# Spreading the taps' weights by transfers and ScalarE copies instead of matmuls, in the first layer of a four-layer network

## The chip, the cores and the metric

The kernel runs on one core of a Trainium2 chip. The metric is the time of one execution on the device, in microseconds (us); the kernel before takes 5737.23 us, the median of three executions (5730.73 to 5739.15).

A core has several engines, each of which works through its own list of instructions in order: TensorE (PE: matmuls into the banks of PSUM), VectorE (DVE), ScalarE (ACT), GpSimd (POOL) and SyncE (SP), which here issues the transfers that the DMA engines carry out. They wait for each other through semaphores. Everything is in float32.

## The reference, cut to what matters

The input x has the shape (2, 512, 64, 64). Four layers follow each other; each adds to x a function of the group-normalized x. Only the first layer is touched by the change. It is an attention in which each of 4096 positions of an image, in each of 8 heads of 64 channels, looks at its 3x3 neighbourhood (9 *taps*) and at 256 pooled tokens:

```python
q_norm = _l2norm(q)
q_scaled = (q_norm + query_embedding[None]) * jax.nn.softplus(temperature)[None]
k_l = _l2norm(k_l.reshape(B, N, nh, hd)).reshape(B, N, C)
# ... k_local, v_local: the 9 shifted images of keys and values
attn_local = jnp.einsum('bhnd,bhndk->bhnk', q_scaled, k_local)
attn_pool = jnp.einsum('bhnd,bhpd->bhnp', q_scaled, _l2norm(k_pool))
attn = jax.nn.softmax(jnp.concatenate([attn_local, attn_pool], axis=-1), axis=-1)
a_local, a_pool = (attn[..., :ll], attn[..., ll:])
lt = jnp.einsum('bhnd,hdk->bhnk', q_norm, learnable_tokens) + learnable_bias[None] + a_local
x_local = jnp.einsum('bhnk,bhndk->bhnd', lt, v_local)
x_pool = jnp.einsum('bhnp,bhpd->bhnd', a_pool, v_pool)
out = ((x_local + x_pool).transpose(0, 2, 1, 3).reshape(B, N, C) @ W_proj + b_proj)
```

Two steps matter here. In x_local each of the 9 weights of a head and a position (lt) multiplies 64 channels of the shifted values, so one row of weights has to be *spread* over 64 partitions. And q and k are divided by their norms, for which 1/sqrt of a sum of squares is needed.

## The kernel before

The first layer works in *units*: two heads (128 channels, one on each partition) by 1024 positions. An image has 4 x 4 = 16 units, both images 32. In each round of the main loop several units are in work at different stages; the stages are Python generators that are advanced in turn, one step of each, and this decides the order of the instructions on every engine:

```python
UT = 2 * TB          # TB = 512: a unit is 1024 positions, two blocks
...
for i in range(-4, units + 1):
    k, q, ahead, u, before = (unit(i + n) for n in (4, 3, 1, 0, -1))
    streams, ended = [], []
    stages = [self.norms(streams, ended)]
    if before is not None:
        stages.append(self.weigh(before))          # apply the taps' weights of the unit before
    if ahead is not None:
        stages.append(self.tap_products(ahead))
    if u is not None:
        stages.append(self.attend(u))              # softmax and pooled part of this unit
    if ahead is not None:
        stages.append(self.tap_sums(ahead))
    stages.append(self.projections(k, q, ahead, streams))
    stages.append(self.normed(ended))
    # ... the output projection, beside the last rounds
    in_turn(*stages)
```

PSUM has a ring of five banks of 128x512 for all these stages ("mm", `self.bank()`), two banks for qs and one for the tap sums.

The attention's stage ends with the reciprocal of the softmax's sums, and the unit's weights are applied in the next round. The spread is a matmul with a matrix of zeros and ones (tapb) from 18 rows of weights to 128 partitions; VectorE multiplies the bank by the shifted values, and GpSimd adds the product to the output:

```python
def attend(self, u):
    # ... exponentials, values, sums (psD) of the unit
    for i in range(2):
        part = slice(i * TB // 2, (i + 1) * TB // 2)
        nc.vector.reciprocal(self.recip[:, part], psD[:, part])
    yield
    yield

def weigh(self, u):
    nc = self.nc
    cc, y0 = u // self.UN, u % self.UN * self.UY
    out, R = self.out.pop(u), self.recip
    el, lt = self.el.pop(u), self.lt.pop(u)
    yield
    banks = [self.bank() for _ in range(2)]
    for j, ps in enumerate(banks):
        q = slice(64 * j, 64 * j + 2)
        nc.tensor.matmul(ps, self.cst[q, C_ROW:C_ROW + P], R[q, :], start=True, stop=True)
    nc.vector.tensor_tensor(el, el, R, ALU.mult)
    nc.vector.tensor_tensor(el, el, lt, ALU.add)
    for j, ps in enumerate(banks):
        o = out[:, j * TB:(j + 1) * TB]
        nc.vector.tensor_tensor(o, o, ps, ALU.mult)
    yield
    for k in range(0, 9, 2):
        banks = {}
        for kk in range(k, min(k + 2, 9)):
            for j in range(2):
                q = 2 * j + kk % 2
                banks[kk, j] = ps = self.bank()
                nc.tensor.matmul(ps, self.tapb[32 * q:32 * q + 18, kk, :],     # L2203
                                 el[32 * q:32 * q + 18, :], start=True, stop=True)
        for (kk, j), ps in banks.items():
            dy, dx = divmod(kk, 3)
            dst = self.weighed[kk % 2]
            y = y0 + dy + j * self.UY // 2
            nc.vector.tensor_tensor(                                           # L2209
                dst[:, j * TB:(j + 1) * TB].rearrange("p (y x) -> p y x", x=W),
                self.vx[:, y:y + self.UY // 2, dx:dx + W],
                ps.rearrange("p (y x) -> p y x", x=W), ALU.mult)
            o = out[:, j * TB:(j + 1) * TB]
            nc.gpsimd.tensor_tensor(o, o, dst[:, j * TB:(j + 1) * TB], ALU.add) # L2214
        yield
        if k < 6:
            yield
    lo = u % self.UN * self.UT
    nc.sync.dma_start(self.yd[:, cc, lo:lo + self.UT], out)
    yield
```

The norms' roots are taken by one instruction on GpSimd, a power of -0.5 on 128x32 elements, once a round:

```python
n = wp.tile([P, NT, 4, 2], F32, name="norms")
nc.vector.tensor_scalar(n, ps.rearrange("p (t s r) -> p t s r", t=NT, s=4)[:, :, :, :2],
                        1e-24, None, ALU.max)                                  # L2012
yield
nc.gpsimd.tensor_tensor(                                                       # L2015
    self.wide.rearrange("p t (s r) -> p t s r", s=4)[:, :, :, :2], n,
    self.half.rearrange("p (t s h) -> p t s h", t=NT, s=4), ALU.pow)
yield
yield
# ... transposes of self.wide, a copy, and the multiplications of q and k
```

Of the kernel before, what the change touches and what calls it, by code (L numbers as in the profile page):

```python
# [8 lines left out]
F32 = mybir.dt.float32  # L9
I32 = mybir.dt.int32  # L10
AF = mybir.ActivationFunctionType
ALU = mybir.AluOpType
# [3 lines left out]
P = 128  # L16
C = 512
KC = C // P
W = 64
N = W * W  # L20
TB = 512
NB = N // TB
NT = TB // P
NH = 8
HD = 64
# [16 lines left out]
def bcast(ap, axis, n):  # L42

    a = ap.unsqueeze(axis)
    shape = list(a.shape)
    shape[axis] = n
    return a.to_broadcast(shape)
# [1612 lines left out]
class Local:  # L1660
# [9 lines left out]
    def __init__(self, net, X, Y, sp_scale, d, wp, yp, pp, ppt, pps):  # L1670
# [5 lines left out]
        self.yd = yp.tile([P, KC, N], F32, name="yd")  # L1676
        self.wd = yp.tile([3, P, KC, C], F32, name="wd")

        R = W + 2
# [5 lines left out]
        weighed = whole.take([P, 2 * self.UT])  # L1685
        self.weighed = [weighed[:, i * self.UT:(i + 1) * self.UT] for i in range(2)]
        self.prods = [whole.take([P, self.UT])] + [new([P, self.UT], f"prod{i}") for i in range(2)]
# [21 lines left out]
        self.sq = [new([P, TB], f"sq{i}") for i in range(4)]  # L1709
        self.tapb = new([P, 9, P], "tapb")  # L1710
        self.half = new([P, 32], "mhalf32")
# [9 lines left out]
        for i in range(2):  # L1721
            load(self.raw_w[i], d["W_kv"][:, i * C:(i + 1) * C])
        nc.sync.dma_start(self.tapb, d["tapb"])
        nc.sync.dma_start(self.tok, d["tok32"])
# [13 lines left out]
    def run(self):  # L1738
# [11 lines left out]
        for i in range(-4, units + 1):  # L1750
            k, q, ahead, u, before = (unit(i + n) for n in (4, 3, 1, 0, -1))
            streams, ended = [], []
            stages = [self.norms(streams, ended)]
            if before is not None:
                stages.append(self.weigh(before))
            if ahead is not None:
                stages.append(self.tap_products(ahead))
            if u is not None:
                stages.append(self.attend(u))
            if ahead is not None:  # L1760
                stages.append(self.tap_sums(ahead))
# [230 lines left out]
    def norms(self, streams, ended):  # L1992
# [15 lines left out]
        for t in range(NT):  # L2008
            nc.tensor.transpose(ps[:, t * P:(t + 1) * P], rows[:, t * P:(t + 1) * P],
                                self.net.ident)  # L2010
        n = wp.tile([P, NT, 4, 2], F32, name="norms")
        nc.vector.tensor_scalar(n, ps.rearrange("p (t s r) -> p t s r", t=NT, s=4)[:, :, :, :2],  # L2012
                                1e-24, None, ALU.max)
        yield
        nc.gpsimd.tensor_tensor(  # L2015
            self.wide.rearrange("p t (s r) -> p t s r", s=4)[:, :, :, :2], n,
            self.half.rearrange("p (t s h) -> p t s h", t=NT, s=4), ALU.pow)
        yield
# [97 lines left out]
    def attend(self, u):  # L2116
# [57 lines left out]
        for i in range(2):  # L2174
            part = slice(i * TB // 2, (i + 1) * TB // 2)
            nc.vector.reciprocal(self.recip[:, part], psD[:, part])
        yield
        yield

    def weigh(self, u):  # L2180

        nc = self.nc
        cc, y0 = u // self.UN, u % self.UN * self.UY
        out, R = self.out.pop(u), self.recip
        el, lt = self.el.pop(u), self.lt.pop(u)
        yield
        banks = [self.bank() for _ in range(2)]
        for j, ps in enumerate(banks):
            q = slice(64 * j, 64 * j + 2)
            nc.tensor.matmul(ps, self.cst[q, C_ROW:C_ROW + P], R[q, :], start=True, stop=True)  # L2190
        nc.vector.tensor_tensor(el, el, R, ALU.mult)
        nc.vector.tensor_tensor(el, el, lt, ALU.add)
        for j, ps in enumerate(banks):
            o = out[:, j * TB:(j + 1) * TB]
            nc.vector.tensor_tensor(o, o, ps, ALU.mult)
        yield
        for k in range(0, 9, 2):
            banks = {}
            for kk in range(k, min(k + 2, 9)):
                for j in range(2):  # L2200
                    q = 2 * j + kk % 2
                    banks[kk, j] = ps = self.bank()
                    nc.tensor.matmul(ps, self.tapb[32 * q:32 * q + 18, kk, :],  # L2203
                                     el[32 * q:32 * q + 18, :], start=True, stop=True)
            for (kk, j), ps in banks.items():
                dy, dx = divmod(kk, 3)
                dst = self.weighed[kk % 2]
                y = y0 + dy + j * self.UY // 2
                nc.vector.tensor_tensor(  # L2209
                    dst[:, j * TB:(j + 1) * TB].rearrange("p (y x) -> p y x", x=W),  # L2210
                    self.vx[:, y:y + self.UY // 2, dx:dx + W],
                    ps.rearrange("p (y x) -> p y x", x=W), ALU.mult)
                o = out[:, j * TB:(j + 1) * TB]
                nc.gpsimd.tensor_tensor(o, o, dst[:, j * TB:(j + 1) * TB], ALU.add)  # L2214
            yield
            if k < 6:
                yield
        lo = u % self.UN * self.UT
        nc.sync.dma_start(self.yd[:, cc, lo:lo + self.UT], out)
        yield  # L2220
# [62 lines left out]
def arrays_of(i):  # L2283
# [49 lines left out]
    for q in range(4):  # L2333
        for h in range(2):
# [4 lines left out]
            == 9 * (p[None, None, :] // HD) + np.arange(9)[None, :, None]).astype(f)  # L2339
    tapb = np.zeros((4, 32, 9, P), f)  # L2340
    tapb[:, :18] = taps.reshape(2, 9, 9, P).transpose(1, 0, 2, 3).reshape(18, 9, P)
    tok = np.zeros((P, KC, 18), f)
# [5 lines left out]
        "vec": vec, "tok": tok,  # L2348
        "taps": taps, "tapb": tapb.reshape(P, 9, P),
        "tok32": np.pad(tok.reshape(P, KC, 2, 9).transpose(0, 1, 3, 2).reshape(P, KC, 18),  # L2350
# [33 lines left out]
```

## Time and profile before

| | before |
|---|---|
| time, median of 3 | 5737.23 us |
| span of the profiled execution | 5739.9 us |
| mean granted TensorE clock | 0.963 |
| moved by DMA | 118.15 MB, mean 21 GB/s |
| a store of a unit's result (yd, 512 KB): to landing | 2.6 us, median |
| a load of the same size from yd | 3.6 to 4.4 us, medians of the groups |
| one load of 2048 KB of x | 9.0 us |

The profile is one execution recorded by the hardware. Its page lists the busy time of each engine, the span in 40 slices, the DMA queues, the chain of work that ended last and the costliest groups of instructions. A group's row names the line of the kernel, the engine, the operation, the tiles written and read (output, arrow, inputs), the shapes and the count; after the first bar stand the busy time in us and the mean of one in ns; after the second the time that the engine was idle just before them, and whose work ended most of it. PEld is the load of a matmul's weights. A float32 matmul of 512 columns leaves two records. Further views give the busy time of each engine in chosen stretches, and the instructions of one engine in order of time (start, duration, engine, line, operation).

The first layer of the first image runs from about 0 to 1190 us of the span: preparation until about 280 us, then the units.

### The profile page before, as it was taken

To read this page: it belongs to the slowest core of one execution; us is meant where nothing else is said; L and a number is where in the kernel's file an instruction comes from. 1 tells how busy PE (TensorE), PEld (TensorE's weight loads), DVE (VectorE), ACT (ScalarE), POOL (GpSimd) and SP (SyncE) were. 2 spreads that over 40 slices of the span, in tenths; PEclk is the share of its full clock that TensorE was granted. 3 is DMA by queue.
4 is the path that set the end of the run, shared out by engine and by line. 5 is a ranking of instruction groups with operands and counts; after the bars stand their busy time and mean duration, and the time that the engine had idled before them with its cause. 6 is when DMAs were issued, how large, how long until landed. Compare 5 with 4: busy or idle time off the path is not lost.

```text
span 5739.9 us, 52308 instructions
## 1 busy us (share of the span) xinstructions
PE 5451.3 (95%) x20443; PEld 2351.5 (41%) x20443; DVE 3020.0 (53%) x3408; ACT 1496.6 (26%) x2837; POOL 2032.2 (35%) x1518
## 2 busy tenths in 40 slices
PE   7899999999988899999998999999999788999999
PEld 4333333455333344544343333334553234445443
DVE  3245655644678733554432555566456696334444
ACT  1233333114212233222212333330242122332221
POOL 0145666510320045443401565664002200454443
PEclk9899999999998999999998999999999899999999
DMA  3000001100000000101010000011000000000000
GB/s 138 0 10 15 13 15 34 59 24 8 16 1 0 1 1 1 74 15 37 30 54 2 8 15 17 15 34 55 24 24 1 1 0 1 1 1 16 21 15 23
DMA packets 52435, 118.15 MB, mean 21 GB/s; under 512 B 4882, under 2 KB 17938, under 8 KB 50132
## 3 DMA queue, kind: packets, MB, share of 16 engines
q1 hardware_dynamic: 52180, 114.72, 5.7%
q8 instruction: 163, 2.67, 0.2%
q14 instruction: 92, 0.75, 0.0%
HBM read 74.86 MB, written 39.85 MB: 20 GB/s over the span
## 4 chain that ended last, share of the span: by engine, by line
PE 66%; DVE 9%; issue 3%; ACT 1%; POOL 1%; DMA 0%; DVEq 0%; ACTq 0%; POOLq 0%; SPq 0%
PE mm L133 19%; DVE big L692 6%; PE mm L1330 4%; PE mm L1615 4%; PE mm L1370 4%; PE mm L547 4%; PE mm L1932 2%; PE mm L1226 2%; PE mm L1410 2%; PE psO L1242 2%; PE psO L1602 2%; PE mm L2203 2%; PE mm L1631 2%; PE mm L2129 1%; PE tap L2097 1%
## 5 line engine op out<-in xcount | busy, mean ns | idle before, releaser
L133 PE MATMUL mm<-big,w 128*128 128x512 f32 x2560 | 1203.6, 615 | 0.0
L2214 POOL TENSOR_TENSOR late<-late,big 128x512 f32<-128x512 f32 x576 | 718.9, 1282 | 374.9 <-DVE big L2209 374.9
L133 PEld LDWEIGHTS mm<-big,w 128*128 128x128 f32 x2560 | 471.5, 194 | 699.0 <-issue 636.5
L1153 PE MATMUL acc<-big,dg 128*128 128x512 f32 x896 | 407.7, 614 | 79.3 <-DVE big L692 51.1
L2209 DVE TENSOR_TENSOR big<-big,mm 128x512 f32<-128x512 f32 x576 | 364.1, 682 | 194.7 <-PE mm L2203 178.0
L692 DVE TENSOR_TENSOR big<-big 128x3968 f32<-128x3968 f32 x96 | 410.8, 4289 | 38.2 <-PE acc L1153 32.7
L1232 POOL TENSOR_TENSOR total<-prob 128x512 f32<-128x512 f32 x128 | 159.8, 1270 | 761.1 <-ACT prob L1229 761.1
L1584 POOL TENSOR_SCALAR qf_sum<-qf,ksum_ratio 128x512 f32<-128x512 f32 x128 | 199.1, 1565 | 552.1 <-ACT qf L1634 351.5
L1405 POOL TENSOR_TENSOR big<-big 128x512 f32<-128x512 f32 x224 | 278.0, 1273 | 234.9 <-ACT big L1396 234.9
L1609 DVE RECIPROCAL k<-psD 128x512 f32<-128x512 f32 x64 | 214.9, 3358 | 185.0 <-PE psD L1606 185.0
L1153 PEld LDWEIGHTS acc<-big,dg 128*128 128x128 f32 x896 | 173.9, 197 | 311.6 <-issue 283.4
L2144 POOL TENSOR_TENSOR late<-late 128x512 f32<-128x512 f32 x128 | 160.2, 1273 | 383.4 <-ACT late L2133 360.4
L2203 PE MATMUL mm<-late,tapb 18*128 18x512 f32 x1152 | 278.2, 635 | 4.4 <-DVE big L2209 3.3
L1396 ACT ACTIVATE big<-mm,ed 128x256 f32<-128x256 f32 x512 | 194.4, 490 | 276.6 <-DVE top L1392 248.8
L1330 PE MATMUL mm<-proj,k 64*128 64x256 f32 x2048 | 265.1, 391 | 0.9 <-ACT k L1297 0.9
L1249 DVE RECIPROCAL recip<-psD 128x512 f32<-128x512 f32 x64 | 214.9, 3358 | 87.1 <-PE psD L1246 87.1
L1330 PEld LDWEIGHTS mm<-proj,k 64*128 64x128 f32 x2048 | 207.5, 188 | 95.1 <-issue 78.7
L1551 DVE TENSOR_REDUCE tops<-mm 128x2 f32<-128x512 f32 x256 | 159.4, 682 | 163.4 <-PE mm L1330 163.3
L2084 DVE TENSOR_TENSOR prod<-qs,big 128x1024 f32<-128x1024 f32 x192 | 231.0, 1216 | 22.2 <-PE tap L2097 22.2
L133 PE MATMUL mm<-big,big 128*128 128x512 f32 x512 | 239.0, 629 | 0.0
L1615 PE MATMUL mm<-k,w 128*128 128x512 f32 x512 | 235.6, 602 | 0.0
L1370 PE MATMUL mm<-w,big 128*128 128x512 f32 x512 | 234.5, 601 | 0.0
(344 smaller groups left out, 7873.8 us busy)
## 6 DMA issues: line engine op xcount, KB each, us to landing
yd<-late SPq DMA_DIRECT2D x32, 512.0 KB, 2.6
out<-big SPq DMA_DIRECT2D x64, 256.0 KB, 2.0
big<-in_W_kv SPq DMA_DIRECT2D x8, 1024.0 KB, 6.0
big<-yd SPq DMA_DIRECT2D x16, 512.0 KB, 3.7
big<-in_x SPq DMA_DIRECT2D x4, 2048.0 KB, 9.0
big<-in_x SPq DMA_DIRECT2D x6, 1024.0 KB, 12.8
wd<-big SPq DMA_DIRECT2D x6, 1024.0 KB, 4.8
w<-wd SPq DMA_DIRECT2D x24, 256.0 KB, 3.0
```

The costliest lines, as they stand in the source:

```text
L133: self.nc.tensor.matmul(ps, w[:, kc, :], X[:, kc, blk * TB:(blk + 1) * TB], start=(kc == 0), stop=(kc == KC - 1))
L547: nc.tensor.matmul(ps, w[:, kc, oc * P:(oc + 1) * P], att[:, kc, :], start=(kc == 0), stop=(kc == KC - 1))
L692: nc.vector.tensor_tensor(o, a, b, ALU.max)
L1153: nc.tensor.matmul(accs[b], dg, src[:, b * TB:(b + 1) * TB], start=(j == 0), stop=(j == 6))
L1330: nc.tensor.matmul(pS[h][i][:, t, :], k[lo:lo + HD, tok:tok + P], proj[lo:lo + HD, :], start=True, stop=True)
L1370: nc.tensor.matmul(ps, X[:, kc, lo:lo + P], wv[:, kc, :], start=(kc == 0), stop=(kc == KC - 1))
L1405: nc.gpsimd.tensor_tensor(a, a, part, ALU.add)
L1615: nc.tensor.matmul(ps, self.wo[:, kc, oc * P:(oc + 1) * P], qs[:, kc, :], start=(kc == 0), stop=(kc == KC - 1))
L2084: self.nc.vector.tensor_tensor(self.prods[k % 3].rearrange("p (y x) -> p y x", x=W), qs, self.kx[:, y + dy:y + dy + self.UY, dx:dx + W], A ...
L2203: nc.tensor.matmul(ps, self.tapb[32 * q:32 * q + 18, kk, :], el[32 * q:32 * q + 18, :], start=True, stop=True)
L2209: nc.vector.tensor_tensor(dst[:, j * TB:(j + 1) * TB].rearrange("p (y x) -> p y x", x=W), self.vx[:, y:y + self.UY // 2, dx:dx + W], ps.re ...
L2214: nc.gpsimd.tensor_tensor(o, o, dst[:, j * TB:(j + 1) * TB], ALU.add)
```

## The change

The taps' weights no longer pass through TensorE. Once a unit's reciprocal is there, the attention's stage itself computes the weights (el), stores them as rows in DRAM (two transfers of 64x512), and starts to fetch tap after tap: for each of its two heads one transfer reads the one row of 1024 weights 64 times and writes it to 64 partitions. There are three buffers for taps in SBUF. ScalarE copies each half of a tap from SBUF into a bank of PSUM, so that VectorE's multiplication still has one operand in PSUM; the product is written over the tap in its buffer. GpSimd adds both blocks in one instruction of 1024 columns, and then the buffer is fetched anew, three taps on.

The norms' power leaves GpSimd: VectorE makes a first guess by a shift and an integer operation on the bits and improves it by three of Newton's steps, 12 instructions on 128x32. The stage that applies the weights moves behind the attention's in the order of the stages. The purpose is to relieve TensorE of the spreading matmuls and GpSimd of the power.

```diff
+        self.rows = cycle([yp.tile([P // 2, self.UT], F32, name=f"rows{i}") for i in range(2)]).__next__
...
-        self.weighed = [weighed[:, i * self.UT:(i + 1) * self.UT] for i in range(2)]
+        self.taps = ([weighed[:, i * self.UT:(i + 1) * self.UT] for i in range(2)]
+                     + [new([P, self.UT], "tap2")])
...
             stages = [self.norms(streams, ended)]
-            if before is not None:
-                stages.append(self.weigh(before))
             if ahead is not None:
                 stages.append(self.tap_products(ahead))
             if u is not None:
                 stages.append(self.attend(u))
+            if before is not None:
+                stages.append(self.weigh(before))
...
-        n = wp.tile([P, NT, 4, 2], F32, name="norms")
+        n, y, a = (wp.tile([P, NT, 4, 2], F32, name=f"norms{i}") for i in range(3))
...
-        nc.gpsimd.tensor_tensor(
-            self.wide.rearrange("p t (s r) -> p t s r", s=4)[:, :, :, :2], n,
-            self.half.rearrange("p (t s h) -> p t s h", t=NT, s=4), ALU.pow)
+        nc.vector.tensor_scalar(y.bitcast(I32), n.bitcast(I32), 1, None, ALU.logical_shift_right)
+        nc.vector.tensor_scalar(y.bitcast(I32), y.bitcast(I32), -1, 0x5f3759df, ALU.mult, ALU.add)
+        nc.vector.tensor_scalar(n, n, -0.5, None, ALU.mult)
+        for i in range(3):
+            nc.vector.tensor_tensor(a, y, y, ALU.mult)
+            nc.vector.tensor_tensor(a, a, n, ALU.mult)
+            dst = self.wide.rearrange("p t (s r) -> p t s r", s=4)[:, :, :, :2] if i == 2 else y
+            nc.vector.scalar_tensor_tensor(dst, a, 1.5, y, ALU.add, ALU.mult)
...
             nc.vector.reciprocal(self.recip[:, part], psD[:, part])
         yield
-        yield
+        el = self.el.pop(u)
+        nc.vector.tensor_tensor(el, el, self.recip, ALU.mult)
+        nc.vector.tensor_tensor(el, el, self.lt.pop(u), ALU.add)
+        self.spread = self.rows()
+        for j in range(2):
+            nc.sync.dma_start(self.spread[:, j * TB:(j + 1) * TB], el[j * HD:(j + 1) * HD, :])
+        self.fetch_tap(0)
+        yield
+        self.fetch_tap(1)
+        yield
+
+    def fetch_tap(self, k):
+        at = 32 * (k % 2) + 2 * k
+        for h in range(2):
+            self.nc.sync.dma_start(self.taps[k % 3][h * HD:(h + 1) * HD, :],
+                                   bcast(self.spread[at + h], 0, HD))
 
     def weigh(self, u):
...
-        el, lt = self.el.pop(u), self.lt.pop(u)
+        self.fetch_tap(2)
         yield
...
-        nc.vector.tensor_tensor(el, el, R, ALU.mult)
-        nc.vector.tensor_tensor(el, el, lt, ALU.add)
...
-        yield
-        for k in range(0, 9, 2):
-            # ... the spreading matmuls, multiplications and additions, as above
+        for k in range(9):
+            dy, dx = divmod(k, 3)
+            parts = [self.taps[k % 3][:, j * TB:(j + 1) * TB] for j in range(2)]
+            banks = [self.bank() for _ in range(2)]
+            for ps, part in zip(banks, parts):
+                nc.scalar.copy(ps, part)
+            for j, (ps, part) in enumerate(zip(banks, parts)):
+                y = y0 + dy + j * self.UY // 2
+                nc.vector.tensor_tensor(
+                    part.rearrange("p (y x) -> p y x", x=W),
+                    self.vx[:, y:y + self.UY // 2, dx:dx + W],
+                    ps.rearrange("p (y x) -> p y x", x=W), ALU.mult)
+            nc.gpsimd.tensor_tensor(out, out, self.taps[k % 3], ALU.add)
+            if k + 3 < 9:
+                self.fetch_tap(k + 3)
+            if k < 8:
+                yield
```

The matrix tapb and its load are gone as well.

## The prediction

> **What bounds the kernel now.** I read the page's busy shares first, then the costliest groups for the lines that the change touches, then the table by stretches for two stretches of the first layer, then the timelines of single engines within one unit.
>
> ```profile
> PE 5451.3 (95%) x20443; PEld 2351.5 (41%) x20443; DVE 3020.0 (53%) x3408; ACT 1496.6 (26%) x2837; POOL 2032.2 (35%) x1518
> ...
> L2214 POOL TENSOR_TENSOR late<-late,big 128x512 f32<-128x512 f32 x576 | 718.9, 1282 | 374.9 <-DVE big L2209 374.9
> ...
> L2209 DVE TENSOR_TENSOR big<-big,mm 128x512 f32<-128x512 f32 x576 | 364.1, 682 | 194.7 <-PE mm L2203 178.0
> ...
> L2203 PE MATMUL mm<-late,tapb 18*128 18x512 f32 x1152 | 278.2, 635 | 4.4 <-DVE big L2209 3.3
> ```
>
> TensorE is busy 95% of the span. The matmuls that spread the taps' weights (L2203) hold it for 278.2 us and find it idle before them for only 4.4 us. L2209 multiplies what they spread by the values on VectorE, and L2214 adds it up on GpSimd. There are 32 units (two images, 16 each), so a unit has 576/32 = 18 spreading matmuls, each with two records.
>
> The stores of a unit's result to yd start at 405.8, 457.8, 511.5, 563.5, 617.2, 669.3, 722.9 us and so on. A pair of units therefore takes 105.7 us, and one 52.9 us. The table by stretches for two such pairs (columns: length, then PE, PEld, DVE, ACT, POOL busy with instructions, granted clock, DMA share, GB/s):
>
> ```profile
> 511.50:617.20 105.70, 105.70 (x401) 35.38 (x400) 60.79 (x76) 33.47 (x54) 65.19 (x46) 0.98 0.04 13
> 617.20:722.90 105.70, 105.70 (x401) 35.47 (x400) 60.78 (x76) 33.46 (x54) 65.20 (x46) 0.98 0.05 18
> ```
>
> TensorE is busy for every microsecond of the pair. Of 52.9 us a unit, VectorE works 30.4, ScalarE 16.7, GpSimd 32.6. The same table for L2203 alone gives 17.19 us a pair, or 8.6 us of TensorE a unit. So in the steady part a microsecond taken off TensorE is a microsecond off the end, until another engine or a wait takes over. The steady part is some 13 units of each image; the last 3 share the time with the output projection, and their TensorE is nearly as full (149.1 of 150 us from 933 to 1083, 104.3 of 107 from 1083 to 1190).
>
> **What the Trainium skill says.** (1) "SBUF — State Buffer", section "Who interferes with whom": a VectorE instruction with two SBUF inputs contends with a GpSimd instruction that reads SBUF, and the second to issue waits for the whole of the first. The trace agrees. The addition of el at L2191 has two SBUF inputs and runs beside GpSimd only sometimes:
>
> ```profile
> L2191 DVE TENSOR_TENSOR late<-late x32: 691/693/1632, 344.6 to 3980.1; 128x512 f32<-128x512 f32 x32
> ```
>
> (minimum, median, maximum in ns). At most it grew by 0.94 us, which is less than one GpSimd addition of 1.28 us. (2) The same page, "Door 1: The DMA port swizzle": 64 partitions reach only half of the ports, 196 GB/s at 1 MiB; and under "Can I just issue two DMAs to hit both halves?" two halves at once gain only 6%. No transfer in this trace fills 64 partitions from one row. (3) "ScalarE: Activation LUTs", "What ACT_TABLE_LOAD costs": an ACTIVATE with immediates takes 186 ns + 0.833 ns for each element of the row, 612 ns for 512. The copy of qs into PSUM in this trace (L2079) takes 589 ns; I use that. (4) "DMA: Bandwidth & Descriptors", "Latency and other measured facts": streams from HBM whose rows collide fell to 103 GB/s. It measures rows at a large pitch, not one row read 64 times, and no run here shows either; it is my yardstick for a bad case.
>
> **The change, part by part, for a steady unit.**
>
> TensorE loses the 18 spreading matmuls: 52.9 - 8.6 = 44.3 us of work are left. Nothing is added to it.
>
> ScalarE gains 18 copies of 128x512 from SBUF to PSUM: 18 x 0.589 = 10.6 us, so 16.7 + 10.6 = 27.3 us.
>
> VectorE keeps its 18 multiplications (one operand still in PSUM, 0.68 us each). It gains Newton's 12 instructions on 128x32. A tensor_scalar of that size takes 192 ns (L2012), a tensor_tensor 185 ns (L1559), so 12 x 0.19 = 2.3 us, and 30.4 + 2.3 = 32.7 us. Nine of the 12 have two SBUF inputs, or work on the same small tiles, and may stand behind a GpSimd addition, which now lasts twice as long. I allow one or two such blocks a unit, about 3 us: 36 us.
>
> GpSimd loses the power on 128x32, shown in its timeline of the unit that starts at 617 us,
>
> ```profile
> 629.33 5.44 POOL L2015 TENSOR_TENSOR wide<-norms,mhalf 128x32 f32<-128x32 f32 x1
> 634.74 9.89 POOL L2214 TENSOR_TENSOR late<-late,big 128x512 f32<-128x512 f32 x8
> ```
>
> and exchanges 18 additions of 512 columns (1.24 us each in a row: 9.89/8) for 9 of 1024. Nothing in the trace has that shape on GpSimd; I take 2 x 1.24 = 2.5 us, no gain. 32.6 - 5.4 = 27.2 us.
>
> The DMA queues gain 9 taps of two 256 KB transfers, that is 4.7 MB a unit or 151 MB in all, more than the 118 MB that the page shows for the whole kernel. Over 44 us this is 107 GB/s, and the issuing queue needs about 20 x 0.33 us (each store to yd holds it 0.32) = 6.6 us. By the table above, at some 200 GB/s and about 2 us fixed, an estimate from the skill's two sections, a tap of 512 KB lands after 2.6 + 2 = 4.6 us. The trace's own loads of 512 KB from yd take 3.6 to 4.4 us, which fits.
>
> So by work alone TensorE still bounds at 44.3 us, with VectorE at 36 next, and the whole change would be worth 32 x 8.6 = 275 us.
>
> What comes back as waits: a tap's buffer passes round a loop, two transfers (about 4.6 us and 0.7 of issuing), two copies on ScalarE (1.2), two multiplications on VectorE (1.4), one addition on GpSimd (2.5), and perhaps 1.5 us of queueing, 11.9 us. With three buffers that is 4.0 us a tap or 36 us a unit. It fits in 44.3 us, but all these engines work in order. When a tap is late, its copy holds up the exponentials behind it on ScalarE, its multiplication holds up the products and Newton's steps on VectorE, and TensorE then finds its five banks taken. The first tap of a unit is tightest: reciprocal 3.4 us, el 1.4, its transfer to DRAM 2.6, the first tap 4.6, together 12 us, and the copy stands some three of ten steps after the reciprocal, 3 x 4.4 = 13 us. I take 3.3 us of stall a unit, chosen between nothing and the whole gain, so 47.6 us and 5.3 us saved. For 26 steady units that is 138 us. In the 6 last units the output's additions already fill VectorE and its loads share the queues; I take 3 us each, 18 us. The sum is 156 us: 5737 - 156 = 5581 us.
>
> **The rivals.**
>
> *Hidden in full.* The waits find slack and TensorE stays full at 44.3 us: up to 275 us, 5462 us. For it speaks that no other engine's sum comes above 36 of 44 us; against it, that the in-order queues today have no DMA in them and now have 18 a unit.
>
> *The row in DRAM is a hot spot.* Sixty-four reads of the same 4 KB, from 16 engines at once, may be slower than a plain load. At the skill's 103 GB/s for colliding streams, 4.7 MB take 46 us and the loop 14 us, so a unit takes about 47 to 50 us and the gain shrinks to 100 to 190 us. At half of that rate a unit takes 92 us, 40 us more than now, and the kernel would lose over 1 ms. Against the worst speaks only that loads here reach 233 GB/s (2048 KB of x in 9.0 us); nothing in the trace reads one row many times.
>
> *VectorE becomes the bound.* If every one of Newton's nine two-input steps waits for a GpSimd addition of 2.5 us, VectorE gets 32.7 + 22 = 55 us a unit, about 2 us more than today: some 60 us slower. Against it: GpSimd is busy 27 of 44 us, and short steps fit between two of its additions.
>
> *Nothing gained.* The spread was also what paced the banks. If each tap's five-engine round costs one long wait, 8 us a unit come back and the time stays within 2%.
>
> **Range and chances.** For 8 times in 10 I take stalls from nearly none (saving 8 us a unit, 5480 us) to all of the gain returned, with slow row reads (5720 us). 2% is 115 us, a saving of 3.6 us a unit. My 5.3 leaves some margin: faster by over 2% 0.6, within 2% 0.25, slower by over 2% 0.15, nearly all of it the hot spot.
>
> **What would show it.** Right: the stores to yd 46 to 49 us apart; no L2203; 576 new copies on ScalarE near 0.59 us; 288 additions of 1024 on GpSimd near 2.5 us; transfers of a tap that land within 5 us; TensorE busy 92 to 95% of a steady stretch, and its idle time put down to VectorE or ScalarE. The DVE steps of Newton at 0.16 to 0.2 us, with a few at 1 us and more. Wrong: transfers that land after 8 us or later would show the hot spot, with GpSimd and ScalarE idle for a DMA; a DVE over 45 us a unit would show the port. A change of more than a few us in the layers after the first would mean that I missed something, since none of their code changes.

## The result, and the profile after

The changed kernel takes 5613.29 us (median; the runs lie between 5603.3 and 5616.7), against 5737.97 us for the kernel before on the same chip: a ratio of 0.978, 95% interval 0.9765 to 0.9799, so 2.2% faster. The profiled executions are 5601.4 and 5739.9 us long, with nearly the same mean TensorE clock (0.962 and 0.963).

The page of the kernel after, with its busy shares, the costliest groups of the first layer (line, engine, operation, tiles and shapes, count | busy us, mean ns | idle time ahead and what ended it), and the transfers (count, KB each, median us to landing):

```profile
PE 5235.5 (93%) x19291; PEld 2262.8 (40%) x19291; DVE 3176.3 (57%) x3816; ACT 1790.9 (32%) x3413; POOL 1811.4 (32%) x1196
...
L2230 POOL TENSOR_TENSOR late<-late,big 128x1024 f32<-128x1024 f32 x192 | 454.0, 2365 | 335.2 <-DVE big L2226 331.7
...
L2223 ACT COPY mm<-big 128x512 f32<-128x512 f32 x384 | 221.7, 594 | 196.6 <-DMA big<-rows 103.3
...
L2226 DVE TENSOR_TENSOR big<-big,mm 128x512 f32<-128x512 f32 x384 | 252.4, 680 | 31.9 <-ACT mm L2223 30.9
...
big<-rows SPq DMA_DIRECT2D x384, 256.0 KB, 4.0
tap<-rows SPq DMA_DIRECT2D x192, 256.0 KB, 4.1
```

The spreading matmuls are gone. In their place stand the ScalarE copies into PSUM (L2223, 0.594 us each), the fetches of the taps (two transfers of 256 KB, landing after a median of 4.0 to 4.1 us) and GpSimd additions of 1024 columns (L2230, 2.365 us). TensorE is now busy 93% instead of 95%, so it no longer fills its time.

Where the time went, by the stores to yd: in the first image, the first store moved from 405.8 to 397.8 us (8.0 us gained), the ten intervals after it shrank from 526.9 to 489.6 us (37.3, or 3.7 each), the last five from 250.1 to 229.6 us (20.5, or 4.1 each), and 2 us came up to the load of the next layer's weights (1215.3 to 1147.6 us). That is 67.7 us in the first image. Up to the same load of the second image it is 136.8 us (4062.4 against 3925.6), of the 138.5 us between the two profiled spans. The layers after it contribute next to nothing, as their code would suggest.

Two pairs of units in the table by stretches (length, then busy PE, PEld, DVE, ACT, POOL with instructions, granted clock, DMA share, GB/s), to be set beside the two pairs of 105.70 us:

```profile
495.93:592.60 96.67, 91.80 (x326) 29.13 (x325) 71.72 (x100) 51.56 (x90) 52.48 (x26) 0.98 0.42 113
592.60:689.25 96.65, 91.69 (x330) 29.50 (x329) 71.72 (x100) 51.65 (x90) 52.49 (x26) 1.00 0.45 123
```

A typical unit takes 48.3 us. Of these TensorE works 45.9, VectorE 35.9, ScalarE 25.8 and GpSimd 26.2. The interesting number is TensorE's: 96.65 - 91.69 = 5.0 us a pair are idle, where before there was nothing.

Where they are is shown by TensorE's timeline of the unit that starts at 592.6 us (start, length, instruction, and in brackets the idle time before it with its releaser):

```profile
605.32 0.62 PE L2104 MATMUL tap<-big,cst 128*32 128x512 f32 x2
605.33 0.62 PE L2104 MATMUL tap<-prod,cst 128*32 128x512 f32 x2
605.77 0.60 PE L2104 MATMUL tap<-big,cst 128*32 128x512 f32 x2
605.78 0.60 PE L2104 MATMUL tap<-prod,cst 128*32 128x512 f32 x2
...
607.37 1.05 PE L2104 MATMUL tap<-prod,cst 128*32 128x512 f32 x2
...
616.36 0.63 PE L2029 MATMUL mm<-cst,wide 128*128 128x128 f32 x4 [2.26 <-DVE wide L2024]
```

The last line is the wait: TensorE stands 2.26 us until L2024, the last of Newton's steps, has written `wide`, which the transposes of the norms read. (The other lines are used further down.) So it isn't the taps that TensorE waits for; it is the root. VectorE's timeline of the same stretch says why:

```profile
606.40 1.27 DVE L2017 TENSOR_SCALAR norms<-norms 128x32 int32<-128x32 int32 x1
...
608.73 1.38 DVE L2018 TENSOR_SCALAR norms<-norms 128x32 int32<-128x32 int32 x1
...
613.08 2.23 DVE L2022 TENSOR_TENSOR norms<-norms,norms 128x32 f32<-128x32 f32 x1
...
616.02 0.19 DVE L2024 SCALAR_TENSOR_TENSOR wide<-norms,norms 128x32 f32<-128x32 f32 x1
```

and beside it GpSimd's:

```profile
605.27 4.80 POOL L2230 TENSOR_TENSOR late<-late,big 128x1024 f32<-128x1024 f32 x2 [0.44 <-DVE big L2226]
612.86 2.41 POOL L2230 TENSOR_TENSOR late<-late,tap 128x1024 f32<-128x1024 f32 x1 [2.78 <-DVE norms L2024]
```

Three of the 12 small steps take 1.27, 1.38 and 2.23 us instead of 0.18 to 0.19. Each of them ends as an addition on GpSimd ends: 606.40 + 1.27 = 607.67 and 605.27 + 2.40 = 607.67; 608.73 + 1.38 = 610.11 and 605.27 + 4.80 = 610.07; 613.08 + 2.23 = 615.31 and 612.86 + 2.41 = 615.27. Together they lose 4.3 us. The whole chain from the clamping of the norms at 605.1 to its end at 616.2 us takes 11.1 us, for 12 x 0.19 = 2.3 us of work; the multiplications and products in between take the rest.

The theory from here on: **Newton's steps stand behind GpSimd's additions, TensorE waits for their end, and that wait eats part of what the taps' matmuls had freed.** Its rivals: the transfers or the copies set the wait; or the work on VectorE as such, blocked or not, is too much.

### The profile page after: what moved, and what is told of

Read it like the earlier page. It is cut to its first block, busy times and chain, and to the rows that moved or that the text cites. A ratio compares the mean times of both kernels' runs of the same rounds, so it can differ in the third digit from the quotient of the medians.

```text
span 5601.4 us, 51804 instructions
## 1 busy us (share of the span) xinstructions
PE 5235.5 (93%) x19291; PEld 2262.8 (40%) x19291; DVE 3176.3 (57%) x3816; ACT 1790.9 (32%) x3413; POOL 1811.4 (32%) x1196
## 4 chain that ended last, share of the span: by engine, by line
PE 72%; DVE 15%; issue 5%; DMA 3%; POOL 2%; ACT 2%; SPq 0%; DVEq 0%; ACTq 0%; POOLq 0%
PE mm L133 25%; DVE big L692 6%; PE mm L1330 4%; PE mm L1615 4%; PE mm L1370 4%; PE mm L547 4%; PE mm L1410 2%; PE mm L1226 2%; PE psO L1242 2%; PE psO L1602 2%; PE mm L1631 2%; PE tap L2104 2%; PE mm L1933 2%; POOL late L2230 2%; DMA big<-rows 2%
## 5 line engine op out<-in xcount | busy, mean ns | idle before, releaser
L2230 POOL TENSOR_TENSOR late<-late,big 128x1024 f32<-128x1024 f32 x192 | 454.0, 2365 | 335.2 <-DVE big L2226 331.7
L2223 ACT COPY mm<-big 128x512 f32<-128x512 f32 x384 | 221.7, 594 | 196.6 <-DMA big<-rows 103.3
L2226 DVE TENSOR_TENSOR big<-big,mm 128x512 f32<-128x512 f32 x384 | 252.4, 680 | 31.9 <-ACT mm L2223 30.9
L2230 POOL TENSOR_TENSOR late<-late,tap 128x1024 f32<-128x1024 f32 x96 | 228.0, 2375 | 122.0 <-DVE norms L2024 72.4
L1229 ACT ACTIVATE prob<-mm 128x512 f32<-128x512 f32 x256 | 132.0, 604 | 364.4 <-PE mm L1226 359.2
```

Source lines behind the costliest of these rows:

```text
L2223: nc.scalar.copy(ps, part)
L2226: nc.vector.tensor_tensor(part.rearrange("p (y x) -> p y x", x=W), self.vx[:, y:y + self.UY // 2, dx:dx + W], ps.rearrange("p (y x) -> p y ...
L2230: nc.gpsimd.tensor_tensor(out, out, self.taps[k % 3], ALU.add)
```

## The experiments

Ratios are to the kernel before, with 95% intervals. Diffs are against the changed kernel unless another is named; they are cut to their core, and `mul(o, a, b)` stands for nc.vector.tensor_tensor(o, a, b, ALU.mult).

**1. The power back on GpSimd.** Everything of the change except Newton's steps.

```diff
-        (12 VectorE instructions: guess and three of Newton's steps)
+        nc.gpsimd.tensor_tensor(wide[..., :2], n, half, ALU.pow)
```

> The whole change except Newton: the norms' roots are again one power on GpSimd (5.44 us, 128x32). The changed kernel takes 5613 us and its TensorE waits about 2.3 us a unit for the last Newton step. Theory N (what TensorE waits for is the length of the roots' chain, which for Newton is 11 us because three steps stood behind GpSimd additions of 2.4 us): the power has to queue among the same additions, 5.4 us plus one or two times 2.4, so its chain is 8 to 10 us, no longer than Newton's; time 5590 to 5650 us. Rival (Newton pays because GpSimd is short of time: 5.4 us more make the tap buffers late): 5660 us or more, with longer waits of the tap transfers for GpSimd.

Measured: 5745.6 us, ratio 1.001 (1.0003 to 1.002). The whole gain is gone, which the theory did not say: taking away the steps that wait made it 132 us slower. ScalarE, GpSimd and TensorE in one unit of this kernel (three views):

```profile
627.54 5.44 POOL L2017 TENSOR_TENSOR wide<-norms,mhalf 128x32 f32<-128x32 f32 x1
```
```profile
640.21 0.59 ACT L2218 COPY mm<-big 128x512 f32<-128x512 f32 x1 [5.53 <-DMA big<-rows]
640.74 0.58 ACT L2026 COPY n_rows<-mm 128x512 f32<-128x512 f32 x1
```
```profile
641.37 2.08 PE L2038 MATMUL mm<-n_rows,cst 2*128 2x512 f32 x4 [4.88 <-ACT n_rows L2026]
...
645.24 5.75 PE L133 MATMUL mm<-big,w 128*128 128x512 f32 x8
```

Read downwards, it is a chain across the engines. The power holds GpSimd for 5.44 us; the additions, and with them the release of the taps' three buffers, come that much later; the next tap is fetched late, and ScalarE waits 5.53 us for it; behind the copy, in ScalarE's order, stands the copy of n_rows; and TensorE waits 4.88 us for that. This is the loop of the prediction (transfer, copy, multiplication, addition), here in the one place where it does not close in time. So moving the power off GpSimd is no small extra: without it the taps' part of the change brings nothing.

The last line shows a second loss. Eight matmul records that take 3.70 us elsewhere take 5.75 us after the gap. The table by stretches of the same kernel gives the granted clock (the column after GpSimd's) around it:

```profile
636.00:638.00 2.00, 0.49 (x4) 0.00 (x0) 0.00 (x0) 0.00 (x0) 1.92 (x2) 1.00 0.70 178
638.00:640.00 2.00, 0.00 (x0) 0.00 (x0) 0.00 (x0) 0.00 (x0) 2.00 (x1) 0.79 0.63 186
640.00:645.00 5.00, 3.63 (x10) 0.70 (x10) 3.94 (x6) 3.22 (x6) 4.20 (x4) 0.50 1.00 222
645.00:650.00 5.00, 5.00 (x10) 2.08 (x8) 3.23 (x4) 0.00 (x0) 3.17 (x2) 0.56 0.50 115
650.00:655.00 5.00, 5.00 (x20) 1.29 (x19) 2.51 (x5) 3.83 (x6) 0.31 (x1) 1.00 0.36 96
```

In the gap the clock falls to half and stays there for some 10 us. The unit takes 54.6 us, longer than before the change. The Trainium skill, "TensorE: Matmul & The Clock Gate", "Part 1: The HAM clock gate", has a rule for this: after an idle window of about 3.4 us TensorE runs at half its clock until it has been busy again for as long. The trace agrees in the fall to 0.50. It does not agree in the return: TensorE works again from 641.4 us on, and the clock is back only at 649.4 us, 8 us later. Tests 5 and 9 ask what it costs.

**2. Newton's steps alone,** on the kernel before (diff against it; y and a lie in unused columns of `wide`):

```diff
-        nc.gpsimd.tensor_tensor(wide[..., :2], n, half, ALU.pow)
+        (the same 12 VectorE instructions)
```

> The kernel before with Newton's steps on VectorE in place of the power, and nothing else (spread still by matmuls, additions of 512 columns). Newton's two temporaries lie in unused columns of the tile wide. TensorE was busy all the time and had no wait for the power to speak of, so by theory N the time stays at 5738 within 15 us, and the blocked steps show as at most 1.3 us each. Rival (Newton is worth something by itself, since GpSimd is freed): 5700 us or less.

Measured: 5777.8 us, ratio 1.006 (1.0044 to 1.008), 37 us slower than the kernel before, which took 5740.7 us beside it, and outside what was expected. VectorE's work rises from 30.4 to 37.0 us a unit, 6.6 us for 2.3 us of instructions. Minimum, median and maximum (ns) of two of the lines:

```profile
L2022 DVE TENSOR_TENSOR wide<-wide,norms x102: 184/1184/1196, 220.8 to 3884.5; 128x32 f32<-128x32 f32 x102
```
```profile
L2017 DVE TENSOR_SCALAR wide<-norms x34: 171/1158/1234, 220.2 to 3876.3; 128x32 int32<-128x32 int32 x34
```

Here with the blocks of the shorter additions, the median step is blocked for 1 us. And it isn't only the steps with two SBUF inputs: L2017, an integer tensor_scalar with one, is blocked as often. So the taps' part of the change and the move of the power need each other: the taps' part without Newton's steps makes +0.1%, Newton's steps alone +0.6%, all together -2.2%.

**3. The steps kept out of GpSimd's way.** The temporaries move into the PSUM bank where the norms arrive; each step then has at most one SBUF input, and no tensor_scalar goes from SBUF to SBUF.

```diff
-        n, y, a = (three tiles in SBUF)
+        v = ps.rearrange("p (t s r) -> p t s r", t=NT, s=4)
+        n, a = v[:, :, :, :2], v[:, :, :, 2:4]      # in PSUM, in place
+        y = wp.tile([P, NT, 4, 2], F32, name="norms")
...
-            mul(a, y, y); mul(a, a, n)
+            mul(a, n, y); mul(a, a, y)
```

> The whole change, but Newton's temporaries n and a stay in the PSUM bank of the transposes, and a = (n*y)*y in place of (y*y)*n, so that no step has two SBUF inputs or SBUF on both sides of a tensor_scalar. Same number of steps. Theory N: no step is blocked (all at 0.17 to 0.2 us), the chain shrinks from 11 to about 4 us, TensorE's 2.3 us of waiting for it vanish in each of 32 units and the products behind it come earlier too: 5490 to 5550 us. Rival (the wait moves to the next late thing, the taps' transfers): 5580 to 5613 us, with the same unit of 48.3 us.

Measured: 5531.5 us, ratio 0.9635 (0.9613 to 0.9658), within the range expected. The steps and one unit of it:

```profile
L2023 DVE TENSOR_TENSOR mm<-mm,norms x102: 190/199/199, 223.3 to 3660.7; 128x32 f32<-128x32 f32 x102
```
```profile
L2018 DVE TENSOR_SCALAR mm<-mm x34: 189/193/200, 218.8 to 3655.5; 128x32 int32<-128x32 int32 x34
```
```profile
582.73:628.60 45.87, 45.75 (x166) 14.76 (x165) 31.72 (x50) 25.85 (x45) 26.20 (x13) 1.00 0.50 128
```

No step of L2023 or L2018 is above 0.20 us, VectorE works 31.7 instead of 35.9 us a unit, and TensorE is busy for 45.75 of 45.87 us. The number and kind of operations is the same; the memory of their operands differs, and the order of two multiplications. That takes 82 us off, against 32 x 2.26 = 72 us of waits. The ten intervals also lost 0.6 us each to the clock, some 12 us in both images, see 9.

**4. No transfers.** Only the first three taps of each image are fetched; all others use what lies in the buffers, so the output is not the reference's and 564 of the 576 transfers are left out.

```diff
     def fetch_tap(self, k):
+        if k > 2 or self.fetched > 2:
+            return
+        self.fetched += 1
```

> The whole change, but only the first three taps of each image are fetched; all later transfers of taps are left out, so the copies, multiplications and additions run on stale data and the output is not the reference's. It shows what waiting for transfers costs. Theory N: little, because ScalarE's waits for a DMA are 1 to 2 us a unit and TensorE waits for a tap's copy under 1 us: 5570 to 5605 us. Rival (the spread row in DRAM and the loop of three buffers hold the kernel back): 5540 us or less.

Measured: 5587.7 us, ratio 0.973 (0.9713 to 0.9751). A steady unit takes 48.3 us with and without the transfers, so in the steady part they cost nothing:

```profile
696.55:744.83 48.28, 45.85 (x166) 14.75 (x165) 35.76 (x50) 25.60 (x45) 26.28 (x13) 1.00 0.05 17
```

All of the gain is made in the last units, where the loads of the output projection share the queues: the last five intervals of the first image take 210.7 instead of 229.6 us, while 7 us are lost ahead of them. In the changed kernel ScalarE waits there, from 940 to 1117 us:

```profile
ACT mm L2223 <- DMA big<-rows: 38.0, 16, 9.2
```

(us in total, times, longest). This rival is a minor one: it falls for the steady unit, and some 12 us an image are left of it in all.

**5 and 9. The gap filled.** To part the wait from its clock, useless matmuls go where TensorE waits in the kernel of test 1 (diff against it; `range(10)`, then `range(5)`):

```diff
+            for _ in range(10 if j else 0):
+                nc.tensor.matmul(psO, ident, X[:, 0, :TB], start=True, stop=True)
```

> The version with the power back (5746 us), and in each unit ten more matmuls of 128x512 whose result is overwritten, put ahead of the second product with the pooled values, so that TensorE has about 4.6 us of idle work where it stood idle for 4.9 us; order, banks and waits of everything else are the same. In that version the granted clock fell to half for about 8 us after each such gap. Theory C (the gap itself costs the clock, and so counts nearly twice): with the gap filled the clock stays at 1.0, a unit takes about 3.9 us less although more is computed, 5600 to 5650 us. Rival (the low clock comes from something else, such as the load of the other engines or the transfers): 5740 us or more.

Measured: 5790.1 us, ratio 1.009 (1.0073 to 1.0106). The dose was wrong: the ten fillers took 8.75 us, where the gap was 4.88, so they added work. The clock did stay at 1.00. With half of them:

> As the run with ten filling matmuls a unit, but five. Ten were too many: they took 8.75 us where the gap was 5 us, so the kernel gained 3.8 us of work a unit and was slower (5790 us), although the granted clock stayed at 1.0 and the units were no longer than without them (54.45 and 54.6 us). Five take 4.4 us and fit. Theory C (an idle gap of 5 us costs the clock as well): clock 1.0 in the units, a unit of 50 to 51 us in place of 54.6, and 5600 to 5660 us in all, though the computed result is the same and more is computed. Rival (the clock was not the gap's doing): 5740 us or more.

Measured: 5692.9 us, ratio 0.991 (0.9895 to 0.9928). The total missed the range, since the fillers also run in the lead-in and in the last units, where they add more than they fill (the first store comes at 407.9 us instead of 395.7). The steady unit is as expected: nine of the ten take 50.6 to 50.9 us, and one 52.4. A unit of test 1, then a unit of this kernel and the fillers in it:

```profile
612.54:667.22 54.68, 49.68 (x166) 15.80 (x165) 30.05 (x38) 25.65 (x45) 31.61 (x14) 0.91 0.42 106
```
```profile
663.08:713.74 50.66, 50.11 (x176) 16.54 (x175) 29.95 (x38) 25.65 (x45) 31.58 (x14) 1.00 0.46 120
...
685.01 4.46 PE L2140 MATMUL mm<-big,cst 128*128 128x512 f32 x10
```

TensorE does 4.46 us of work for nothing, and the unit is 54.68 - 50.66 = 4.0 us shorter. Its other matmuls, the same in both kernels, take 50.11 - 4.46 = 45.65 us here and 49.68 in test 1. The time that they leave in a unit is the same: 5.0 us idle there, 4.46 us of fillers and 0.55 idle here. So the 4.0 us are clock (1.00 against 0.91): in the kernel of test 1 the low clock costs nearly as much as the gap.

Does the changed kernel suffer from it too, with gaps of 2.26 us? Mostly not: the clock of the second pair above is 1.00. But the unit from 689 to 742 us takes 53.1 us, and the stretches of it show why:

```profile
710.00:715.00 5.00, 2.74 (x18) 1.00 (x12) 4.86 (x8) 2.83 (x6) 1.92 (x1) 0.94 0.34 98
715.00:720.00 5.00, 5.00 (x14) 0.70 (x10) 4.09 (x7) 1.77 (x4) 4.59 (x3) 0.50 0.22 66
720.00:725.00 5.00, 5.00 (x9) 2.04 (x7) 3.26 (x4) 0.00 (x0) 4.89 (x3) 0.54 0.38 111
725.00:730.00 5.00, 5.00 (x20) 1.17 (x18) 2.48 (x4) 3.69 (x6) 0.16 (x1) 1.00 0.53 150
```

After the gap that ends at 713.0 us the clock is at half for some 10 us. One more of the ten intervals shows it, 49.8 us long with a clock of 0.97. The ten are therefore 48.96 us long on average, and not 48.33.

The gaps of all ten are alike, 2.26 to 2.27 us; what differs is where they lie. Read in finer stretches, the clock falls at 567.6, 714.4 and 912.4 us, that is at distances of 43 and 58 times 3.413 us, and the low stretches last 3.4, 10.2 and 13.7 us, whole multiples of the same 3.41 us. If the time is cut into such steps, TensorE is idle for 2.27, 2.02 and 2.16 us of the step ahead of these three falls. Between 397.8 and 940.5 us the other gaps are split by a border between two steps, so that at most 1.79 us lie in one. In this profile, then, a gap of 2.3 us costs the clock only when at least 2.0 us of it fall into one step. That is read from the trace; no run here shifts the gaps to test it.

**6. One block per addition.** Only the part "two blocks per addition" is undone: each product is added as soon as it is there.

```diff
-            nc.gpsimd.tensor_tensor(out, out, self.taps[k % 3], ALU.add)
+                o = out[:, j * TB:(j + 1) * TB]
+                nc.gpsimd.tensor_tensor(o, o, part, ALU.add)
```

> The whole change, but GpSimd adds each block of 512 columns by itself (18 additions of about 1.25 us instead of 9 of 2.37), as before. Theory N: Newton's steps are then blocked for at most 1.3 us each instead of 2.2, but by more additions, so the chain is a little shorter or the same; GpSimd works 1 us more a unit. 5580 to 5640 us, near the 5613 of the whole change. Rival (two blocks per addition are what lets GpSimd keep up): over 5660 us.

Measured: 5533.7 us, ratio 0.964 (0.9623 to 0.9655), better than expected. Without touching Newton's steps the longest block is halved, and so is the wait:

```profile
653.64 0.63 PE L2029 MATMUL mm<-cst,wide 128*128 128x128 f32 x4 [0.91 <-DVE wide L2024]
```

0.91 us instead of 2.26, the clock stays at 1.00 in the unit, and it takes 46.95 us. GpSimd works 27.8 us a unit instead of 26.2, in time that it has. In the first image 19.8 us are gained in the ten intervals and 13.2 in the last five. This part of the change thus costs 80 us beside Newton's steps in SBUF; what it saves, 1.6 us of GpSimd a unit, nobody waits for.

**7. Newton's steps alone, kept out of the way:** test 2 with the steps of test 3.

> The kernel before, with Newton's steps in place of the power in the form that keeps n and a in PSUM. Newton alone in its SBUF form made that kernel slower by 0.6% (5778 us). Theory N (the 0.6% are steps blocked behind GpSimd, 37.0 instead of 30.4 us of VectorE a unit): all steps at 0.2 us, TensorE full again, 5725 to 5745 us. Rival (twelve more instructions on VectorE cost this by themselves): 5765 us or more.

Measured: 5747.7 us, ratio 1.0015 (1.0008 to 1.0022). VectorE works 32.2 us a unit instead of 37.0. Of the 37 us that the steps cost in test 2, 29 were blocks. What remains is under 0.2%, just above the range that was expected. The rival that the work as such is too much for VectorE falls.

**8. No copies into PSUM.** The kernel of test 3 with the multiplication straight from the tap in SBUF (diff against it):

```diff
-            banks = [self.bank() for _ in range(2)]
-            for ps, part in zip(banks, parts):
-                nc.scalar.copy(ps, part)
...
-                    ps.rearrange(...), ALU.mult)
+                    part.rearrange(...), ALU.mult)
```

> The version with Newton in PSUM (5531 us), but without ScalarE's 18 copies a unit: VectorE multiplies the tap from SBUF by the values from SBUF, and the taps take no banks. Theory N (two SBUF inputs stand behind a running GpSimd addition): of the 18 multiplications many wait for up to 2.4 us, VectorE works over 40 us a unit, and the kernel is slower than 5531: 5570 to 5700 us. Rival (the copies are only there by habit; banks and ScalarE are worth more): 5530 us or less.

Measured: 5608.7 us, ratio 0.977 (0.9754 to 0.9787), 77 us more than with the copies. Minimum, median and maximum (ns) of the multiplications:

```profile
L2223 DVE TENSOR_TENSOR big<-big x384: 622/691/2851, 354.4 to 3909.0; 128x512 f32<-128x512 f32 x192
L2223 DVE TENSOR_TENSOR tap<-big,tap x192: 623/878/2880, 361.2 to 3912.7; 128x512 f32<-128x512 f32 x192
```

With two SBUF inputs they are blocked for up to 2.3 us, and VectorE's work rises to 40.2 us a unit. A copy costs 0.594 us on ScalarE, which has time to spare, and keeps VectorE out of this. The blocks need not be the whole of the 77 us: without the copies it is VectorE that waits, in its order, for the taps' transfers (18.5 us in the two units from 594.4 us on), and this run does not part the two.

**10. Tests 3 and 6 together.**

> Newton in PSUM (5531 us) and GpSimd's additions by blocks of 512 (5534 us) together. If both of them took away the same thing, Newton's steps standing behind long additions (theory N), the two do not add up: 5515 to 5535 us. Rival (the halved additions have a gain of their own, a block can be added while the other is still multiplied and the tap's buffer is free earlier): 5500 us or less, mostly in the last units.

Measured: 5509.7 us, ratio 0.960 (0.9584 to 0.9616), between the two answers. A steady unit is 45.9 us, as in test 3: with no step to block, the length of an addition no longer matters there. The 22 us more come from the lead-in (first store at 392.4 instead of 398.8 us) and the last five intervals (212.4 instead of 221.3 us).

**11 and 12. The order of the tap sums.** TensorE's own work in test 3 is 45.75 us a unit, not 44.3. The tap sums alone (busy PE, PEld), in a pair of units of the changed kernel and in one of the kernel before:

```profile
592.60:689.25 96.65, 14.33 (x72) 2.44 (x72) 1.00 0.45 123
```
```profile
617.20:722.90 105.70, 10.79 (x72) 1.55 (x72) 0.98 0.05 18
```

Before the change the same 72 records took 10.79 us. The matmuls are the same; the first TensorE timeline above shows the difference. Each fills 32 of the 128 partitions of its bank, and the four of two taps run side by side: from 605.32 to 606.38 eight records take 1.06 us. At 607.37 two records stand alone between other matmuls and take 1.05 us as well. The change moved a stage in the order, and with it such groups were split. First try: within the kernel of test 10, swap the two taps of a group, to bring neighbours together.

```diff
-            sums(k)
             sums(k + 1)
+            sums(k)
```

> As the version with both, and the tap sums of the second tap of a pair are issued ahead of the first's. In the changed kernel the tap sums take TensorE 7.2 us a unit, in the kernel before 5.4, with the same matmuls: four of them, of 32 columns each in four quadrants, run side by side when they follow each other (8 records in 1.0 us), and in the changed order two of them stand alone (2 records in 1.05 us). Theory G: with this order they stand in fours again except for one pair, the tap sums fall to about 6 us or below and a unit by 1 to 1.7 us: 30 to 50 us less than the version it is built on. Rival (TensorE waits for the products anyway): within 10 us of it.

Measured: 5534.8 us, ratio 0.964 (0.9621 to 0.9654): 25 us slower than test 10. The edit did not bring the groups together (the tap sums still take 7.16 us a unit, as in test 3), so it says nothing about their cost. Most of what it loses lies in the last five intervals, 225.6 us at a clock of 0.95 against 212.4 us at 0.98 in test 10. Second try, the order of the stages (against test 10):

```diff
-             if before is not None:
-                 stages.append(self.weigh(before))
              stages.append(self.projections(k, q, ahead, streams))
              if ahead is not None:
                  stages.append(self.tap_sums(ahead))
+             if before is not None:
+                 stages.append(self.weigh(before))
```

> The version with Newton in PSUM and additions by 512 (5510 us), with the stages in another order: projections ahead of the tap sums, and the stage that applies the weights after both. The tap sums then stand in fours on TensorE nearly everywhere (112 groups of four in the program, against 62 before this edit, and 10 single ones against 52), as in the kernel before. The run that only swapped the two taps of a pair had not brought them together and was slower. Theory G (tap sums that stand alone cost TensorE 1.75 us a unit): tap sums back to about 5.4 us a unit, a unit of about 44.2 us in place of 45.9, and 5455 to 5490 us. Rival (the later stage makes taps late, and what is saved is waited): a unit of 46 us or more, 5510 us or more.

Measured: **5494.7 us, ratio 0.957 (0.9554 to 0.9586)**, faster than both kernels, though just short of the range expected. The tap sums, then all engines, of the same pair of units:

```profile
527.96:616.62 88.66, 10.62 (x74) 1.55 (x72) 1.00 0.50 131
```
```profile
527.96:616.62 88.66, 88.24 (x330) 28.61 (x328) 67.02 (x100) 51.60 (x91) 55.70 (x44) 1.00 0.50 131
```

The sums are back at 10.6 us a pair and TensorE's work at 44.1 us a unit. In this pair it is full again (88.24 of 88.66 us). This is what the matmuls' removal could bring in the steady part. The ten intervals average 44.8 us, though: TensorE waits six times in them for the copy of n_rows, for up to 1.4 us, and one unit of 47.4 us has a clock of 0.96. The last five intervals are 3.5 us longer than in test 10. So the gain over test 10 is 15 us and not 20 or more.

## Why the prediction was right

The time, 5613 us, lies inside the range, 32 us above the figure named, and the direction was the likelier one. By its own steps:

**The work of the engines** was sized well. VectorE: 36 us a unit said, 35.9 measured; ScalarE 27.3 and 25.8; GpSimd 27.2 and 26.2, with 2.365 us for the addition that I had put at 2.5; the copy 0.589 and 0.594 us.

**"Nothing is added to it"** (TensorE) failed. Its instructions were counted right, but not their neighbours: the split tap sums cost (14.33 - 10.79)/2 = 1.8 us a unit. 44.3 + 1.8 = 46.1, and 45.9 was measured. Test 12 brings the groups together again and comes to 44.1.

**The transfers** were right: 4.6 us said for a tap, 4.0 to 4.1 measured. The rival of a hot spot is refuted; 64 partitions reading one row are no slower than a plain load, and test 4 puts their steady cost at nothing.

**The stall of 3.3 us a unit** was chosen, not derived, and its cause was a different one. I had the taps' loop in mind, with Newton's steps as a term of about 3 us on VectorE's work. The loop closes in time (test 4); the blocked steps lose 4.3 us, of which 2.26 arrive at TensorE. Test 3 removes them and the wait goes. All in all TensorE is idle for 2.5 us a unit, less than the 3.3 that I chose, and has 1.6 us more to do than I said. The two errors work against each other, so that the typical unit comes within 0.7 us of mine is in part luck. The sign that I named, a few of Newton's steps at 1 us and more, was there; what I did not see is that they lie on TensorE's path, since the transposes wait for the last of them. The rival that VectorE becomes the bound had the right mechanism and the wrong size: three steps a unit wait, not nine, and VectorE stays at 35.9 of 48.3 us.

**The sum.** Per image I had 13 units at 5.3 us and three at 3, 78 us; measured were 67.7 in the first image. The term that was off is the 5.3: the ten intervals gave 3.73 each. The difference of 1.6 us is the typical unit (48.33 instead of 47.6, 0.7 us), the clock after some of the gaps (48.96 - 48.33 = 0.6 us), of which the prediction knew nothing, and the unit before, 52.7 us on average and not 52.9 (0.2 us). The last five gave 20.5 us where my terms give 2 x 5.3 + 3 x 3 = 19.6, and the first store 8.0 us where they give 5.3.

**What I would not have guessed** from the page is how the parts depend on each other. The relief of GpSimd is what lets the taps' loop close (test 1), and adding two blocks at once, which looks like a saving, costs 80 us beside Newton's steps in SBUF (test 6) and 22 beside those in PSUM (test 10).

What stays open: why the last units of test 11 lose more to the clock than those of test 10, why the copy of n_rows comes late in some units of test 12, and how much of test 8 is blocks.

## What to carry to other kernels

When work moves from GpSimd to VectorE, look not at its sum but at who waits for its last step, and at which of its operands lie in SBUF while GpSimd works: putting temporaries in PSUM cost nothing and gave 82 us. Longer instructions on GpSimd save little and block longer, so merge them only where nobody beside them can be blocked. And when a stage is moved in an in-order queue, compare the busy time of matmuls that did not change: small ones that ran side by side may no longer be neighbours.

## What the runs showed of the hardware

- A VectorE instruction with a single SBUF input, an integer tensor_scalar on 128x32 from SBUF to SBUF, waits for GpSimd's addition to end (1.27 to 1.38 us instead of 0.18); with input and output in PSUM it takes 0.19 us. The prediction counted only on the steps with two SBUF inputs. The Trainium skill has both cases ("SBUF — State Buffer", "Who interferes with whom": tensor_scalar can enter modes that take the shared ports), and the trace agrees.
- An idle gap of TensorE can cost twice: in and after one of 4.88 us the clock is at 0.50 for about 10 us, worth 4.0 us a unit. Gaps of 2.26 us, shorter than the 3.4 us of the Trainium skill ("TensorE: Matmul & The Clock Gate", "Part 1: The HAM clock gate"), did so in two of ten units, where at least 2.0 us of them fell into one step of 3.41 us.
- Two 32-column matmul records alone take 1.05 us, eight that run side by side 1.06 us.
- A power on 128x32 holds GpSimd for 5.44 us, more than two additions of 1024 columns.
